# Expert groups of a Flamingo layer: rows turned by the vector engine, odd halves in threes, and the experts' choice and bias additions moved

## The chip, the cores and the metric

The kernel runs on one core of one Trainium2 chip. The metric is the device time of one execution in microseconds (us); the kernel before was timed nine times. The engines are named as the profile names them: PE is the tensor engine's matmuls and PEld its weight loads, DVE the vector engine, ACT the scalar engine, POOL GpSimd, SP the engine that issues most DMAs. All data are 32-bit floats.

## The reference

The layer has two parts, each with a gated residual; x is 8 batches of 512 tokens of 256 features.

```python
x = x + tanh(g_xattn) * (attention(layernorm(x), ctx, ctx, mask) @ wo.T + bo)   # 16 heads of 16
x = x + tanh(g_ffn)   * experts(layernorm(x))

# experts: 8 of them, 256 -> 1024 -> 256, the best 2 of a token
probs = softmax(x_flat @ router_w + router_b)        # 4096 tokens x 8
top_w, top_idx = top_k(probs, 2)
comb = sum(top_w[..., None] * one_hot(top_idx, 8), axis=1)
for e in range(8):
    h = gelu(x_flat @ expert_up[e].T)                # exact gelu
    output += comb[:, e:e+1] * (h @ expert_down[e].T)
```

The mask leaves only the last keys of a sequence open; the kernel reads from the mask that they fit into a window of 128 keys, and then takes the branch `attend_near`. Everything below is about this branch; for any other mask a general branch stands beside it.

## The kernel before, in words

**One schedule for two parts.** `attend_near` (L830) runs the attention batch by batch and mixes the expert layer into it. A batch has four quarters g, and each quarter three slots n: slot 0 weighs the values of the quarter before (`weigh`, L925), slot 1 finds the largest scores for the batch after (`find_tops`, L876), slot 2 lowers queries by them (`lower_tops`, L897). Around these, `between` (L969) fills a plan of (g, n) with the steps of the batches before and after: output projection (`project_out`, L950), layer norms, keys, values and queries. The instructions of an engine run in the order in which the steps issue them; a step waits where its data is not there. The loop is at L1062 to L1101.

**A weighing.** PE multiplies the weights with the values (L933), DVE transposes the result into `raw` (L939), divides it (`n_o`, L942) and, in every second quarter, transposes the heads' outputs (`oT`, L947), which PE projects (L954). GpSimd adds the output bias to a batch's x (`add_bias`, L866): at (2, 0) of the plan, for the first two batches at (1, 0) and (1, 2). `scale_out` (L853) makes that bias once: two columns of `bvT` are spread over 128 by DVE (`bv_rows`, L860) and multiplied with `woT` by PE (L861).

**The choice of experts.** For a finished batch `logits` (L314) multiplies with the router; `route` (L326 to L356), some 25 small DVE operations, takes the softmax and the best two; `place` (L359) counts on GpSimd where each choice goes in a table in memory that has a stretch for every expert; `enter` (L392) scatters the entries (token to read, token to write, weight) by eight indirect DMAs. `route` is at (3, 2); `place` and the scatters follow in the next batch from (0, 2) on. `plan` (L624) turns counts into groups: for each group an expert and a line of the table. Its parts need 3, 6, 8 and 8 finished batches.

**The groups.** A pair is 256 rows of one expert, a single 128. There are 32 pairs (5 + 12 + 15 by part), 4 singles between the last pairs, and 4 more singles in a conditional block. So 36 groups, if the block is not taken. For each group s: SP reads its list from the table (`list_rows`, L707) and its weights, 1 MB up and 1 MB down (`load`, L719); GpSimd gathers its rows (`fetch`, L735), by one indirect DMA per 128 rows; PE turns them by four 128x128 transposes into PSUM and DVE copies that to `xT` (`turn`, L741); PE multiplies with the up weights, two of eight blocks of 128 features at a time, with a Gelu on ACT for each two (`go_up`, L751). `fetch_y` (L764) gathers what the output holds so far for these rows, `go_down` (L770) multiplies with the down weights, adds on DVE (L779) and scatters the rows to the output (L782), one half of 128 rows after the other. Since a token has two experts, the gather of a group's y waits for the scatter of the group before.

**Order of a group.** `compute` (L793) writes group s's steps out: gather of the rows of s + 2, gather of y of s - 1, ups of s, turning of s + 1, downs of s - 1, the list of s + 3, the weights of s + 2. Groups 0 to 3 are worked in amid the attention (`amid`, L1038); from group 4 on the groups run one after the other, each step followed by one of a queue (L1103 to L1114) that holds the last batches' projection, choice, places and scatters.

Of the kernel before, what the change touches and what calls it, by code (L numbers as in the profile page):

```python
# [35 lines left out]

TOKENS = B * S
GROUP = 2 * P
PAIRS = 2 * TOKENS // GROUP
SINGLES = E  # L40

TABLE = TOKENS // GROUP


PARTS = (3, 6, B, B)
ENDS = [-(-(b * S * 2 - E * (GROUP - 1)) // GROUP) for b in PARTS[:2]] + [PAIRS]
SIZES = [ENDS[0], ENDS[1] - ENDS[0], ENDS[2] - ENDS[1], SINGLES]

OFTEN = SINGLES // 2

TABLES = E * TABLE + SIZES[2]
# [4 lines left out]
for _n in range(SIZES[2]):  # L56
    JOBS.append((2, _n))
    if _n % 3 == 2 and _n // 3 < OFTEN:
        JOBS.append((3, _n // 3))
MAIN = len(JOBS)  # L60
JOBS += [(3, n) for n in range(OFTEN, SINGLES)]
# [3 lines left out]
def flamingo_layer(ctx: ExitStack, tc: tile.TileContext, a: dict, out: bass.AP):  # L65
# [11 lines left out]
    table = tc.dram_tile([TABLES * GROUP, ENTRY], I32, name="table")  # L77

    table_parts = dram_disjoint_views(table, B * QT * 2)
    out_parts = dram_disjoint_views(out, 2)  # L80
# [73 lines left out]
    def clear_table(t):  # L154

        many = t.rearrange("p (n c) -> p n c", c=ENTRY)[:, : TABLES * GROUP // P // 11]
        nc.gpsimd.memset(many, 0)
        nc.gpsimd.memset(many[:, :, 0], TOKENS)
        nc.gpsimd.memset(many[:, :, 1], TOKENS - 1)
        n = many.shape[1]  # L160
        nc.sync.dma_start(
            out=table.rearrange("(p r n) c -> p r (n c)", p=P, n=n),
            in_=t[:, : n * ENTRY].unsqueeze(1).to_broadcast([P, TABLES * GROUP // P // n, n * ENTRY]),
        )
# [8 lines left out]
    full_i = mk.tile([P, 2 * TABLE], I32, tag="full_i", name="full_i")  # L173
    nc.gpsimd.iota(full_i, pattern=[[P, 2 * TABLE]], base=0, channel_multiplier=0)
    full = fixed([P, 2 * TABLE], "full")
# [13 lines left out]
    nc.vector.tensor_scalar(filled, iota, float(TOKENS), None, ALU.mult)  # L189
# [422 lines left out]
    def experts(pool, seen, half_bank, bank, row_bank):  # L612
# [6 lines left out]
        tables, loaded, fetched, turned, made, ys = {}, {}, {}, {}, {}, {}  # L619

        def halves(s):
            return 1 if JOBS[s][0] == 3 else 2

        def plan(k):  # L624
            n = SIZES[k]
            single = k == 3
            w = 1 if single else 2
            lines = 2 * TABLE // w

            def planned(shape, name, dtype=F32):  # L630
                return plans.tile(shape, dtype, tag=f"{name}{k}", name=f"{name}{k}")

            def scratch(shape, name):
                return plans.tile(shape, F32, tag=name, name=f"{name}{k}")

            def count():

# [3 lines left out]
                count = scratch([P, E], "count")  # L641
                nc.vector.scalar_tensor_tensor(count, iota, -float(TOKENS), filled, ALU.mult, ALU.add)
                if not single:
                    nc.vector.tensor_scalar(count, count, 1.0 - GROUP if k < 2 else -float(P), None, ALU.add)
                more = scratch([P, E, lines], f"more{lines}")
                nc.vector.tensor_tensor(
                    more, count.unsqueeze(2).to_broadcast([P, E, lines]),
                    full[:, ::w].unsqueeze(1).to_broadcast([P, E, lines]), ALU.is_gt,
                )
                groups = scratch([P, E + 1], "groups")  # L650
                nc.vector.memset(groups[:, E:], 0.0)
                nc.vector.tensor_reduce(groups[:, :E], more, AX.X, ALU.add)
                if k:
                    nc.vector.scalar_tensor_tensor(groups, tables["done"], -2.0 / w, groups, ALU.mult, ALU.add)
                ahead = scratch([P, E + 1, E], "ahead")
                nc.vector.tensor_tensor(
                    ahead, lower, groups[:, :E].unsqueeze(1).to_broadcast([P, E + 1, E]), ALU.mult
                )
                begin = scratch([P, E + 1], "begin")
                nc.vector.tensor_reduce(begin, ahead, AX.X, ALU.add)  # L660

                line = scratch([P, E + 1], "line")
                nc.vector.scalar_tensor_tensor(line, iota_e, float(lines), begin, ALU.mult, ALU.subtract)
                if k:
                    nc.vector.scalar_tensor_tensor(line, tables["done"], 2.0 / w, line, ALU.mult, ALU.add)
                past = scratch([P, n, E + 1], f"past{n}")
                nc.vector.tensor_tensor(
                    past, slot[:, :n].unsqueeze(2).to_broadcast([P, n, E + 1]),  # L670
                    begin.unsqueeze(1).to_broadcast([P, n, E + 1]), ALU.is_ge,
                )
                whose = scratch([P, n], f"whose{n}")
                nc.vector.tensor_reduce(whose, past, AX.X, ALU.add)
                whose_i = planned([P, n], "whose_i", I32)
# [10 lines left out]
                else:  # L686
# [4 lines left out]
                    if k:  # L691
                        nc.vector.tensor_tensor(done, done, tables["done"], ALU.add)
# [684 lines left out]
    with which.Else():  # L1377
        with ExitStack() as att:
            attend_anywhere(att)
        with ExitStack() as exp:  # L1380
# [7 lines left out]
            for count in plans:  # L1388
                count()
# [53 lines left out]
```

## Time and profile before

| what | value |
|---|---|
| time, median of nine (lowest to highest) | 843.58 us (838.62 to 850.68) |
| the profiled execution: its own time, its span | 840.35 us, 838.6 us |
| PE busy in the span | 767.6 us (92%) |
| DVE, ACT, POOL busy | 321.8, 255.3, 312.9 us |
| matmuls down (L776) and up (L758) | 244.1 and 243.9 us |
| transposes of rows (L746), 136 | 21.2 us |
| moved by DMA | 121.58 MB, 145 GB/s |

A line of a timeline has the start and the length in us, the engine, the line of the kernel, the operation, its output and inputs, its shape and how many instructions stand together (x32); in brackets is the idle time of the engine ahead of it and what ended that. Matmuls are pipelined, so neighbouring lengths overlap a little: the pace is read from start to start. The granted clock is the share of full speed that PE was given. Releasers are inferred; an engine's idle time costs something only where a later thing waits for that engine.

The span has three stages: the attention alone (to about 215 us), the attention with groups 0 to 3 between its steps (to about 461 us, with the last batches' remainder at its end), and the groups alone.

### The profile page before, as it was taken

Reading aid. Unit: us, or ns where it says so; the run is one execution under the profiler, and the core shown is the slowest. Engines: PE = TensorE matmul, PEld = TensorE weight load, DVE = VectorE, ACT = ScalarE, POOL = GpSimd, SP = SyncE. Lnnn points to the kernel's source line nnn. Section 1 sums busy time; section 2 is a strip of 40 time slices with the busy share of each in tenths; the row PEclk is TensorE's granted clock in tenths of the full one; section 3 lists DMA queues with packets and bytes.
Section 4 is the critical chain, followed back from the end, with each engine's and each line's share of the span. In section 5 each row is a group of like instructions: output and inputs, shape, how many; then the busy total and the mean of one; then the engine's idle time right before and its main releaser. Section 6 shows DMA issues by size and latency. Waiting matters only on the chain.

```text
span 838.6 us, 11329 instructions
## 1 busy us (share of the span) xinstructions
PE 767.6 (92%) x4090; PEld 568.1 (68%) x4090; DVE 321.8 (38%) x958; ACT 255.3 (30%) x487; POOL 312.9 (37%) x420
## 2 busy tenths in 40 slices
PE   4989989897999999899996999999999999999992
PEld 1443544444456656668785888888898988988882
DVE  6856977878774665632220111111011101101100
ACT  3554636363645344432311111111111111111210
POOL 2030123334453251635463444343343333433332
PEclk9988979999989999999999999999999999999997
DMA  4700202010662223254548466665666765756511
GB/s 153 254 7 2 67 21 79 4 51 4 225 217 85 82 71 109 65 165 142 164 142 301 157 208 214 191 222 173 229 193 211 243 221 178 260 182 224 195 51 36
DMA packets 87909, 121.58 MB, mean 145 GB/s; under 512 B 16797, under 2 KB 71712, under 8 KB 87840
## 3 DMA queue, kind: packets, MB, share of 16 engines
q1 hardware_dynamic: 75184, 93.44, 33.6%
q0 software_dynamic: 11840, 26.76, 10.2%
q8 instruction: 36, 0.59, 0.3%
q10 hardware_dynamic: 816, 0.53, 0.2%
q14 instruction: 33, 0.27, 0.1%
HBM read 101.05 MB, written 20.17 MB: 145 GB/s over the span
## 4 chain that ended last, share of the span: by engine, by line
PE 27%; DMA 12%; issue 8%; POOL 3%; DVE 0%; SPq 0%; POOLq 0%; DVEq 0%
PE o_ps L776 14%; PE h_ps L758 12%; DMA out<-y,listed 5%; DMA y<-out,listed 5%; POOL out L782 1%; POOL y L730 1%; PE x_ps L746 1%; DMA xg<-rows,listed 1%; POOL xg L730 1%; DVE y L779 0%; DMA table<-entries,place_i 0%; DMA listed<-table 0%; POOLq L782 0%; POOL filled L371 0%; POOL place L370 0%
## 5 line engine op out<-in xcount | busy, mean ns | idle before, releaser
L776 PE MATMUL o_ps<-down,hT 128*128 128x256 f32 x1088 | 244.1, 382 | 11.2 <-DVE y L779 10.0
L758 PE MATMUL h_ps<-xT,up 128*128 128x256 f32 (+1 forms) x1152 | 243.9, 368 | 3.5 <-DMA up<-in_upT 1.8
L776 PEld LDWEIGHTS o_ps<-down,hT 128*128 128x128 f32 x1088 | 204.9, 191 | 43.7 <-DVE y L779 11.5
L758 PEld LDWEIGHTS h_ps<-xT,up 128*128 128x128 f32 x1152 | 208.1, 190 | 34.0 <-issue 4.9
L762 ACT ACTIVATE hT<-h_ps 128x512 f32<-128x512 f32 (+1 forms) x144 | 82.0, 573 | 366.1 <-PE h_ps L758 298.2
L779 DVE SCALAR_TENSOR_TENSOR y<-o_ps,listed,y 128x256 f32<-128x256 f32 x68 | 32.6, 482 | 278.3 <-DMA y<-out,listed 128.6
L730 POOL DMA_INDIRECT y<-out,listed x68 | 66.2, 974 | 155.8 <-DMA out<-y,listed 125.7
L782 POOL DMA_INDIRECT out<-y,listed x68 | 68.9, 1013 | 109.9 <-DVE y L779 84.1
L890 DVE TENSOR_REDUCE tops<-t_ps 128x4 f32<-128x512 f32 x128 | 79.1, 680 | 17.1 <-PE t_ps L885 13.8
L920 ACT ACTIVATE n_pT<-w_ps 128x512 f32<-128x512 f32 x128 | 68.2, 596 | 53.6 <-PE w_ps L915 31.9
L730 POOL DMA_INDIRECT xg<-rows,listed x68 | 65.3, 960 | 41.7 <-issue 16.9
L394 POOL DMA_INDIRECT table<-entries,place_i x64 | 62.9, 982 | 25.9 <-issue 16.4
L748 DVE COPY xT<-x_ps 128x512 f32<-128x512 f32 (+1 forms) x36 | 23.7, 658 | 105.3 <-PE x_ps L746 95.2
L915 PE MATMUL w_ps<-ql,km 32*128 32x512 f32 x256 | 58.6, 694 | 1.8 <-DVE tops L890 1.8
L885 PE MATMUL t_ps<-k,q 32*128 32x256 f32 x512 | 42.8, 405 | 3.1 <-issue 1.2
L954 PE MATMUL proj_ps<-woT,oT 128*128 128x256 f32 x128 | 35.6, 418 | 9.8 <-DVE oT L947 9.8
L885 PEld LDWEIGHTS t_ps<-k,q 32*128 32x128 f32 x512 | 26.2, 184 | 24.8 <-issue 14.7
L867 POOL TENSOR_TENSOR x<-x,bo 128x1024 f32<-128x1024 f32 x8 | 18.9, 2372 | 61.6 <-issue 33.6
L933 PE MATMUL n_av<-n_pT,nv 128*32 128x512 f32 x256 | 38.1, 671 | 2.4 <-DVE xT L748 2.3
L939 DVE STREAM_TRANSPOSE raw<-n_av 128x512 f32<-128x512 f32 x32 | 22.8, 712 | 44.4 <-PE n_av L933 26.3
L954 PEld LDWEIGHTS proj_ps<-woT,oT 128*128 128x128 f32 x128 | 24.8, 205 | 21.4 <-DVE oT L947 11.4
L553 PE MATMUL q_ps<-n_xnT,wqT 128*128 128x512 f32 x64 | 33.3, 645 | 0.8 <-ACT n_xnT L282 0.5
(187 smaller groups left out, 549.8 us busy)
## 6 DMA issues: line engine op xcount, KB each, us to landing
up<-in_upT SPq DMA_DIRECT2D x36, 1024.0 KB
down<-in_downT SPq DMA_DIRECT2D x36, 1024.0 KB
out<-x SPq DMA_DIRECT2D x8, 512.0 KB
rows<-xn_f SPq DMA_DIRECT2D x8, 512.0 KB
x<-in_x SPq DMA_DIRECT2D x7, 512.0 KB
table<-none SPq DMA_DIRECT2D x1, 2288.0 KB
xg<-rows,listed POOLq DMA_INDIRECT x68
y<-out,listed POOLq DMA_INDIRECT x68
```

What stands on the lines that cost most here:

```text
L394: nc.gpsimd.indirect_dma_start(out=table_parts[2 * t + i][:, :], out_offset=bass.IndirectOffsetOnAxis(ap=place_i[:, t, i : i + 1], axis=0) ...
L730: nc.gpsimd.indirect_dma_start(out=dst, out_offset=None, in_=src[: seen[JOBS[s][0]], :], in_offset=bass.IndirectOffsetOnAxis(ap=listed[:, ...
L758: nc.tensor.matmul(ps[:, i, :n], lhsT=up[:, dc, (f + i) * P : (f + i + 1) * P], rhs=xT[:, dc, :n], start=(dc == 0), stop=(dc == DC - 1),)
L762: nc.scalar.activation(made[s][:, f : f + 2, :n], ps[:, :, :n], AF.Gelu)
L776: nc.tensor.matmul(ps, lhsT=hT[:, f, h * P : (h + 1) * P], rhs=down[:, f, :], start=(f == 0), stop=(f == FC - 1))
L782: nc.gpsimd.indirect_dma_start(out=out_parts[h][:, :], out_offset=bass.IndirectOffsetOnAxis(ap=listed[:, n, h, 0:1], axis=0), in_=y[:, h, ...
L885: ins = nc.tensor.matmul(ps[j][:, u], lhsT=q[rows_j, c, t * P : (t + 1) * P], rhs=k[rows_j, c], start=True, stop=True)
L890: nc.vector.tensor_reduce(top[:, 2 * tp : 2 * tp + 2, :].rearrange("p t (i x) -> p t i x", i=2)[:, :, :, 32 * j], ps[j], AX.X, ALU.max,)
L915: ins = nc.tensor.matmul(ps[j], lhsT=km[rows_j, c, i, :], rhs=lowered[b, c][rows_j, i, :], start=True, stop=True)
L920: nc.scalar.activation(pT[:, j, :], ps[j], AF.Exp)
L933: ins = nc.tensor.matmul(av[32 * j : 32 * j + 32, :], lhsT=made_of(b)[3][:, 8 * c + 2 * j + r, :], rhs=pT[:, j, :], start=True, stop=True,)
L954: nc.tensor.matmul(ps[:, t - ts[0], :], lhsT=outs[b, c][:, t * P : (t + 1) * P], rhs=w["woT"][:, c, :], start=(c == 0), stop=(c == DC - 1),)
```

## The change

- **Rows turned by DVE.** From group 4 on the rows are no longer turned by PE. `turn_block` makes `xT` by DVE's 32x32 transposes from `xg` straight, in four steps of four instructions, each from 32 partitions to 32 others; the steps are put after the first four ups of the group before. Groups 0 to 3 keep `turn`. The conditional blocks turn their first group by PE.
- **Odd halves in threes.** Singles are gone. An expert's odd half goes with one of its last pairs as a triple of 384 rows; there are four triples, in a pool `wide` that is opened when the queue is empty and the heads' pools are closed. `plan_rest` counts these and the last pairs together, from all 8 batches. The main line has 5 + 12 + 11 pairs and 4 triples; three and four more pairs stand in two nested conditional blocks. A triple's ups go one block of features at a time, with eight Gelus. The table has lines of 128 rows, and the output is written through three views rather than two.
- **The choice a quarter on.** `route` goes from (3, 2) to (0, 2) of the next batch, `place` and the scatters (with the plan behind them) from (0, 2) to (1, 2) on; in the queue at the end likewise.
- **The bias.** `add_bias` first issues a DVE copy of a column of `bo` onto itself, held in the program's order, which the addition on GpSimd waits for; it goes from (2, 0) to (3, 0), the second batch's from (1, 2) to (2, 0). `scale_out` gives PE the column of `bvT` spread by its access pattern, without DVE's two operations.
- **The last group.** Its predecessor's downs come after its first two ups, rather than after all.

```diff
-PAIRS = 2 * TOKENS // GROUP
-SINGLES = E
...
+TRIPLES = 4
+HALVES = TOKENS // P
+SHARE = HALVES + 1
...
+SIZES = [ENDS[0], ENDS[1] - ENDS[0], TRIPLES, 2 * TOKENS // GROUP + E - 1 - TRIPLES - ENDS[1]]
+OFTEN = SIZES[3] - 7
+MORE = OFTEN + 3
...
+LINES = E * SHARE + 2 * SIZES[3]
...
+for _n in range(OFTEN):
+    JOBS.append((3, _n))
+    if _n % 3 == 1 and _n // 3 < TRIPLES:
+        JOBS.append((2, _n // 3))
...
-    out_parts = dram_disjoint_views(out, 2)
+    out_parts = dram_disjoint_views(out, 3)
...
+            pairs, whole = each("pairs"), each("whole")
+            nc.vector.tensor_reduce(pairs, more[:, 0], AX.X, ALU.add)
+            nc.vector.tensor_reduce(whole, more[:, 1], AX.X, ALU.add)
+            left, odd = each("left"), each("odd")
+            nc.vector.tensor_tensor(left, pairs, tables["done"][:, :E], ALU.subtract)
+            nc.vector.tensor_tensor(odd, pairs, whole, ALU.subtract)
...
+            three = each("three")
+            nc.vector.scalar_tensor_tensor(three, left, 2.0, odd, ALU.is_ge, ALU.mult)
+            some, two = each("some"), each("two")
+            nc.vector.tensor_scalar(some, left, 1.0, None, ALU.is_ge)
+            nc.vector.tensor_tensor(two, some, three, ALU.subtract)
...
+            groups = scratch(3, [P, E + 1], "groups")
+            nc.vector.tensor_tensor(groups[:, :E], left, saved, ALU.subtract)
+            begin = plan_pairs(3, groups)
+            for i, end in enumerate((OFTEN, MORE)):
+                tables["extra", i] = planned(3, [P, 1], f"extra{i}_", I32)
+                nc.vector.tensor_scalar(tables["extra", i], begin[:, E:], float(end), None, ALU.is_gt)
...
+        def rows_for(s, name, bufs=None):
+            w = halves(s)
+            if w == 3:
+                return wide[0].tile([P, w, D], F32, tag=f"{name}3", name=f"{name}{s}")
+            return gather.tile([P, w, D], F32, tag=name, name=f"{name}{s}", bufs=bufs)
...
+        def turn_block(s, i):
+            w = halves(s)
+            if i == 0:
+                where, bufs = (wide[0], 1) if w == 3 else (gather, 2)
+                turned[s] = where.tile([P, DC, w * P], F32, tag="xT" if w == 2 else "xT3", name=f"xT{s}", bufs=bufs)
+            src = fetched[s].rearrange("p h (k g x) -> p g k h x", k=DC, x=32)
+            dst = turned[s].rearrange("p k (h i r) -> p i k h r", h=w, r=32)
+            for g in range(4):
+                nc.vector.transpose(dst[32 * g : 32 * g + 32, i], src[32 * i : 32 * i + 32, g])
...
+            m = 512 // (halves(s) * P)
+            return [lambda f=f: go_up(s, f, m) for f in range(0, FC, m)]
...
         def downs(s):
             return [lambda h=h: go_down(s, h) for h in range(halves(s))]
@@ -795,11 +895,17 @@
             steps = [lambda: fetch(s + 2)] if s + 2 < end else []
             if s > first:
                 steps.append(lambda: fetch_y(s - 1))
-            steps += ups(s)
+            up = ups(s)
+            last = downs(s - 1) if s > first else []
             if s + 1 < end:
-                steps.append(lambda: turn(s + 1))
-            if s > first:
-                steps += downs(s - 1)
+                turned_next = turns(s + 1)
+                for step in up:
+                    steps += [step, *turned_next[:1]]
+                    turned_next = turned_next[1:]
+                steps += turned_next + last
+            else:
+                steps += up[:2] + last + up[2:]
...
             for c in range(DC):
-                rows_c = small.tile([P, P], F32, tag="lgT", name=f"bv_rows{c}", bufs=1)
-                tc.keep_in_program_order(nc.vector.tensor_scalar(rows_c, ones, bvT[:, c : c + 1], None, ALU.mult))
-                nc.tensor.matmul(bias_ps, lhsT=rows_c, rhs=w["woT"][:, c, :], start=(c == 0), stop=(c == DC - 1))
+                nc.tensor.matmul(
+                    bias_ps, lhsT=bvT[:, c : c + 1].to_broadcast([P, P]), rhs=w["woT"][:, c, :], start=(c == 0),
+                    stop=(c == DC - 1),
+                )
...
         def add_bias(b):
+            tc.keep_in_program_order(nc.vector.tensor_copy(bo[:, :1], bo[:, :1]))
             nc.gpsimd.tensor_tensor(xs[b], xs[b], bo.unsqueeze(1).to_broadcast([P, QT, D]), ALU.add)
...
-                    put(1, 2, lambda: add_bias(1))
+                    put(2, 0, lambda: add_bias(1))
                 if new > 1:
-                    put(2, 0, bias)
+                    put(3, 0, bias)
             if next_ is not None:
...
-                put(3, 2, route)
...
-            + [lambda: load(5), lambda: turn_rows(4)],
+            + [lambda: load(5), *turns(4)],
...
-            for place, enter, counts in behind_route:
-                plan[0, 2].append(place)
+            for route, place, enter, counts in behind_route:
+                plan[0, 2].append(route)
+                plan[1, 2].append(place)
                 if counts:
-                    plan[0, 2] += enter + counts
+                    plan[1, 2] += enter + counts
                 else:
-                    for where, step in zip(((0, 2), (1, 0), (1, 1), (1, 2)), enter):
+                    for where, step in zip(((1, 2), (2, 0), (2, 1), (2, 2)), enter):
                         plan[where].append(step)
             for g in range(4):
...
-        (place, enter, _), (last, enter_last, counts) = later
-        mixed = [step for pair in zip(rest, [place, *enter] + [wait] * len(rest)) for step in pair]
+        (route, place, enter, _), (route_last, last, enter_last, counts) = later
+        mixed = [step for pair in zip(rest, [route, place, *enter] + [wait] * len(rest)) for step in pair]
         spread = [step for one in enter_last for step in (one, wait, wait)]
-        queue = deque([*mixed, wait, last, *spread, *counts])
+        queue = deque([*mixed, route_last, last, *spread, *counts])
         for s in range(DONE, MAIN):
             for step in compute(s, MAIN, DONE):
                 step()
                 if queue:
                     queue.popleft()()
+                    if not queue:
+                        heads.close()
+                        open_wide()
         compute_extra()
 
 
```

`plan_rest` in short: from the counts it takes, per expert, `pairs` (groups of 256 begun) and `whole` (groups of 256 full over the half), `odd = pairs - whole`, `left = pairs - done`; experts that are odd and have two or more pairs left come first for the four triples, then others with any left; a triple of an odd expert takes the place of two pairs begun. The other pairs are laid out as in `plan` before, now in `plan_pairs`.

## The prediction

> **What bounds the kernel now.** I read the page's engine shares and its 40 slices first, to learn which engine is full and when; then the busy time per stage; then the timeline of TensorE (PE) in the expert stage, for the price of one group; and last the stretches where PE stands still, with the engine that it waits for.
>
> ```profile
> PE 767.6 (92%) x4090; PEld 568.1 (68%) x4090; DVE 321.8 (38%) x958; ACT 255.3 (30%) x487; POOL 312.9 (37%) x420
> ...
> PE   4989989897999999899996999999999999999992
> ```
>
> PE is full from the 23rd slice on, and nearly so from the 11th. By stage (columns: stretch, length, then busy time of PE, PEld, DVE, ACT, POOL, the granted clock, DMA share, GB/s):
>
> ```profile
> 0.00:215.00 215.00, 181.38 (x1053) 89.65 (x1053) 167.03 (x499) 104.27 (x215) 54.57 (x101) 0.93 0.20 65
> 215.00:461.00 246.00, 227.41 (x1282) 162.17 (x1281) 113.20 (x381) 92.69 (x168) 110.90 (x169) 0.97 0.46 148
> 461.00:824.00 363.00, 358.79 (x1756) 316.33 (x1756) 41.08 (x78) 58.37 (x104) 145.36 (x148) 1.00 0.59 195
> ```
>
> In the last stage only 4.2 us are not PE's, so only less PE work shortens it, and DVE has 322 us to give. In the first, PE and DVE lean on each other. PE's timeline (start, length, work, idle before it and what ended that):
>
> ```profile
> 461.04 8.82 PE L776 MATMUL o_ps<-down,hT 128*128 128x256 f32 x32 [6.27 <-DVE y L779]
> ...
> 491.30 7.07 PE L776 MATMUL o_ps<-down,hT 128*128 128x256 f32 x32
> 498.21 7.07 PE L758 MATMUL h_ps<-xT,up 128*128 128x256 f32 x32
> 505.12 0.60 PE L746 MATMUL x_ps<-ident,xg 128*128 128x128 f32 x4
> 505.55 7.07 PE L776 MATMUL o_ps<-down,hT 128*128 128x256 f32 x32
> ...
> 681.84 3.72 PE L776 MATMUL o_ps<-down,hT 128*128 128x256 f32 x16 [1.41 <-DVE y L779]
> ```
>
> From one group's downs to the next's are 14.25 us: 6.91 downs, 6.91 ups, 0.43 for the four transposes of the rows. That last is what the change takes from PE.
>
> **The rows turned by DVE.** The 36 groups hold 68 halves of 128 rows. By the router's counts, worked out from the reference's inputs, the new groups hold 68 too (28 pairs, 4 triples), the seven conditional groups not run. Groups 0 to 3, pairs, keep PE's transposes: 60 halves × 0.216 us (0.43 / 2) = **−12.9**, all on the full engine. DVE gets 16 transposes of 32 partitions × 128 elements per pair, and loses a copy of 0.69. No row has 32 partitions. Nearest: a 128x512 transpose (0.71) above, a 128x4 reciprocal (0.18) below, a 128x128 DVE operation between (0.28, L860). With the elements per partition deciding, I take 0.29: 4.6 us per pair, and 0.97 for its two y additions, within the 13.82 that PE leaves. The cover is gone where 16 of them exceed 12.85, at 0.80 each. The transposes wait for the gathered rows (xg), and behind them on DVE's queue stand the y additions; rows gathered a group ahead leave some 20 us before anybody lacks them.
>
> The Trainium skill ("VectorE: DVE Perf Modes", section "Rules for kernel authors") speaks against this step: a 128×128 transpose belongs on TensorE, since DVE's transposes only 32×32 blocks. The trace's row agrees on PE's cheapness (0.108 us a block) but shows PE full and DVE idle; by the rule this step would be worth nothing or less and the sum would be 12.9 higher.
>
> **The loop through memory.** A group's y is gathered from the output after the previous group's scatter has landed; without PE's transposes this loop has less room.
>
> ```profile
> 513.43 1.01 POOL L782 DMA_INDIRECT out<-y,listed  x1 [1.85 <-DVE y L779]
> 519.79 0.98 POOL L730 DMA_INDIRECT y<-out,listed  x1 [5.36 <-DMA out<-y,listed]
> ...
> 523.64 0.48 DVE L779 SCALAR_TENSOR_TENSOR y<-o_ps,listed,y 128x256 f32<-128x256 f32 x1 [2.94 <-DMA y<-out,listed]
> ```
>
> An addition ending at 513.14 lets the next group's first start at 523.64, 10.5 us later; the second half's gather is issued 1.29 later (521.08), so 11.8, and with 0.8 for the addition and its release 12.6 in all. The room is 13.82: it fits, by 1.2. POOL's six issues are 6 × 1.27 = 7.6. So I cost it at nothing.
>
> **Odd halves in threes.** A single's ups take 3.57 us where half a pair's take 3.46: 4 × 0.11 = **−0.45**. After singles PE waits for the loop: 1.41 (681.84), 0.63 (768.65), 1.23 (784.40), in all 3.27. A triple has 20.7 us for its loop: **−3.3**. Eight Gelus a triple are beside other work, as are the plan's some 40 DVE operations of about 0.2 (as in the choice's rows), 8 us once where DVE has 1 busy us in 9; the wider tiles take the place of the heads' long before the first triple; four groups fewer load 8 MB less.
>
> **The tail.** The last addition (824.40) stood 0.65 for its y, and the last scatter leaves at 826.47, 3.4 after PE's end (823.1). With the previous downs moved in after the first two ups, the last y is there before PE ends: about 0.9 remain, **−2.5**; the 11.1 us from that issue to the end stay.
>
> **The attention part.** Three times PE stands 3.07 us for oT (117.23, 157.41, 196.71):
>
> ```profile
> 117.23 2.93 PE L954 MATMUL proj_ps<-woT,oT 128*128 128x256 f32 x6 [3.07 <-DVE oT L947]
> ```
>
> ```profile
> 109.54 0.18 DVE L330 TENSOR_TENSOR lg<-lg_ps,rb 128x32 f32<-128x32 f32 x1
> ...
> 113.83 2.60 DVE L942 TENSOR_TENSOR n_o<-raw,inv 128x256 f32<-128x256 f32 x1
> 116.47 0.71 DVE L947 STREAM_TRANSPOSE oT<-n_o 128x512 f32<-128x512 f32 x1
> ```
>
> ```profile
> 113.81 2.34 POOL L867 TENSOR_TENSOR x<-x,bo 128x1024 f32<-128x1024 f32 x1 [1.49 <-ACT xn_a L271]
> ```
>
> Two causes lie on DVE's queue ahead of oT: the choice of experts (109.54 to 112.88, 3.35 us), which the change moves a quarter on, and n_o, which took 2.60 beside the bias addition and 0.42 elsewhere (105.47), the addition being what the gate shifts. The Trainium skill ("SBUF — State Buffer", section "SBUF: two separate sides") calls the port pair of DVE and GpSimd an exclusive lock for operations with two SBUF inputs; the rows agree: n_o starts 0.02 us after the addition and lasts as long. After the stall the granted clock is 0.59 from 114 to 126 us and the six projections take 2.93 where at full clock (1.56) 1.4 less; over the three I read some 3 us. scale_out's matmul waits 2.62 for the first of its two DVE operations at 48.81. Gross: 9.2 + 3.0 + 2.6 = 14.8. Against it: the moved choice stands ahead of the next quarter's tops and lowered queries, for which the w_ps matmuls wait; walking DVE's queue on, I get about 1.2 us in each of three batches, 3.6; and with DVE busy 167 of 215 us part of the rest comes back as another wait for it. Ends: 0 (the stall only changes its place) and −18 (that gross and the low clock of 45 to 80 us as well). I take **−8**, near the middle, as the 2.45 us of four tops now met are nearly as large as the wait removed. The gate is a DVE copy of one column, at most 0.18 (the smallest tensor row), 8 × 0.18 = 1.4 on DVE; what queues behind it are that quarter's tops, and it waits only if the bias addition before it, 2.34 us and a quarter or a batch earlier, is unfinished: nothing.
>
> **The place in the table, moved too.** The table's scatters, eight issues of 1.27, go a quarter (about 10 us) later, and POOL's order with them: gathers of rows and y stand behind them, and SP's queue holds the weights' loads behind lists that wait for them. In the first batches there is room: first list 216.0, first rows used 239.67. At the passage to the expert stage there is none: 6.27 (461.04), 1.82 (447.19, weights) and 0.50 idle, 8.6 in all. There the choice moves too. Ends: −8.6 (all gone) and +4 (half a loop of waiting more). My walk of POOL's new order has y of group 6 some 7 us late, yet its PSUM bank free 2.5 us before PE needs it. I take **−2.5**.
>
> **Sum** against the profiled execution, 840.35 us (span 838.6): −12.9 −0.45 −3.3 −2.5 −8 −2.5 = −29.6, so 810.7. The median of nine, 843.58, stands 3.2 above that execution; added: **814**. This kernel's times tell about 0.5%, 4.2 us, from no change.
>
> **The rivals.**
> B, the loop through memory becomes the bound: the gather's landing, now beside DVE's transposes and a denser PE, takes 1.65 us longer than the 12.6, and the pace stays 14.25. For it: room of 1.2 only. Against: POOL's issues keep 0.95 to 1.02 whatever DVE does. 814 + 12.9 = 827.
> C, the moves in the attention part don't do what they say: PE waits for tops at w_ps as long as it did for oT, and the passage costs 4 more. 814 + 8 = 822; with the passage 828, and with each of three batches losing the whole 3.35 of the choice anew 838. Speaks for it: DVE's share there.
> D, the other side: DVE becomes the bound of the expert stage. A pair costs DVE 16t + 0.97, and 24 pairs past group 3 have 13.82. The other steps give 29.6, so slower than before from 24 × (16t − 12.85) = 29.6, t = 0.88 us a transpose. At 0.9, 37 us: 851. Speaks for it: no row of this shape, and that the 128x512 transpose costs 0.71 says that a form can be dear; against: that row is a whole bank in less than 0.80.
> E, more: the passage's stall goes wholly (6.1 more) and the attention part gives its 15 (7 more): 801.
>
> **How the numbers follow.** Forecast 0.55 (own range 806 to 820), B 0.12, C 0.15, D 0.09, E 0.09. The range 799 to 835 leaves out D, C's upper end and what exceeds E. Faster: 0.55 + 0.12 + 0.09 + 0.11 of C = 0.87; the same: C's other 0.04; slower: D, 0.09.
>
> **What would show it.** No x_ps matmuls past group 3, and 13.8 us from downs to downs. Transposes from xg on DVE near 0.3 us each; over 0.8, D. An idle time of PE ended by y's addition in each group: B. In the first 215 us, the waits of 3.07 for oT gone and n_o at 0.42 throughout; waits at w_ps for tops above 3 us instead: C. The idle time near 461 tells the passage; the last scatter within 1 us of PE's end the tail. A conditional group run would cost a pair, 14 us, and would make all this wrong.

## The result, and the profile after

The changed kernel takes 884.0 us (median of 20 runs, 876.6 to 889.6) where the kernel before, in 62 runs beside it, takes 841.8: a ratio of 1.051, 95% interval 1.049 to 1.053. It is slower by 42 us, and the forecast of 814, with a range to 835, is wrong in sign. The profiled execution took 885.17 us with a span of 883.5.

The page of the changed kernel, the lines that answer to those shown of before:

```profile
PE 761.6 (86%) x3842; PEld 547.8 (62%) x3842; DVE 431.5 (49%) x1390; ACT 257.6 (29%) x489; POOL 312.8 (35%) x420
...
PE   4999988788899898496979999986959977996993
```

PE has 248 instructions fewer, as it should, and DVE 110 us more work, at 49% still far from full. But PE, which was full from the 23rd slice on, now has a hole of 4 tenths in the 17th and others down to 5 tenths from the 28th on, nearly to the end. The stages (stretch, length, busy time of PE, PEld, DVE, ACT, POOL, granted clock, DMA share, GB/s):

```profile
0.00:215.00 215.00, 182.57 (x1113) 89.26 (x1117) 163.15 (x517) 111.21 (x230) 52.32 (x100) 0.94 0.21 68
215.00:461.00 246.00, 209.41 (x1151) 149.75 (x1144) 132.92 (x472) 85.29 (x151) 108.60 (x165) 0.93 0.40 135
461.00:824.00 363.00, 325.56 (x1401) 273.28 (x1400) 131.12 (x393) 54.81 (x96) 136.01 (x139) 0.95 0.52 171
```

The first stage does more work than before in the same time (1113 matmuls for 1053). In the second and third, which are the same stretches of time as before and not the same work, PE is busy for 18 and 33 us less, at a lower clock. What PE waited for (engine, line, releaser: us in total, times, the longest):

```profile
PE o_ps L872 <- DVE y L875: 42.5, 8, 9.7
PE xnT_ps_f L283 <- DVE y L875: 11.8, 1, 11.8
...
PE lg_ps L330 <- DVE y L875: 7.2, 1, 7.2
```

All three end with the addition of y on DVE: 42.5 + 11.8 + 7.2 = 61.5 us. In the kernel before, the waits for y were 10.3 us (the line below, and 0.3 in one other):

```profile
PE o_ps L776 <- DVE y L779: 10.0, 5, 6.3
```

PE's timeline of the changed kernel shows where:

```profile
485.69 7.07 PE L872 MATMUL o_ps<-down,hT 128*128 128x256 f32 x32
492.60 7.07 PE L854 MATMUL h_ps<-xT,up 128*128 128x256 f32 x32
499.50 7.07 PE L872 MATMUL o_ps<-down,hT 128*128 128x256 f32 x32
...
585.32 8.86 PE L872 MATMUL o_ps<-down,hT 128*128 128x256 f32 x32 [2.77 <-DVE y L875]
...
608.74 9.36 PE L872 MATMUL o_ps<-down,hT 128*128 128x256 f32 x32 [7.65 <-DVE y L875]
617.94 10.48 PE L854 MATMUL h_ps<-xT,up 128*128 128x384 f32 x32
```

Between 472 and 575 us a pair takes 13.81 us, as forecast. The stalls begin when DVE comes to the first triple's transposes, ahead of that triple's ups (128x384), and come again at the transposes of each other triple (9.23 us at 658, 9.71 at 734, 7.25 at 807). The larger ones are followed by matmuls at a lower clock: 9.36 us for work of 7.07 at 608.74, where the granted clock is 0.76, against 1.00 from 472 to 575 us. The other two waits, 11.8 and 7.2 us, end at 372 and 415 us, where DVE holds transposes of groups 5 and 7. Why the addition is late is seen on DVE and on GpSimd, at the first triple:

```profile
569.71 4.11 DVE L843 STREAM_TRANSPOSE xT<-xg 32x128 f32<-32x128 f32 x13
584.00 0.75 DVE L843 STREAM_TRANSPOSE xT<-xg 32x192 f32<-32x192 f32 x2 [10.18 <-DMA xg<-rows,listed]
584.78 0.48 DVE L875 SCALAR_TENSOR_TENSOR y<-o_ps,listed,y 128x256 f32<-128x256 f32 x1
585.30 4.58 DVE L843 STREAM_TRANSPOSE xT<-xg 32x192 f32<-32x192 f32 x12
589.91 0.48 DVE L875 SCALAR_TENSOR_TENSOR y<-o_ps,listed,y 128x256 f32<-128x256 f32 x1
```

```profile
572.57 0.99 POOL L807 DMA_INDIRECT y<-out,listed  x1 [6.62 <-DMA out<-y,listed]
573.86 0.97 POOL L807 DMA_INDIRECT y<-out,listed  x1 [0.30 <-issue]
575.14 0.95 POOL L807 DMA_INDIRECT xg<-rows,listed  x1 [0.30 <-issue]
576.40 0.95 POOL L807 DMA_INDIRECT xg<-rows,listed  x1 [0.30 <-issue]
577.65 0.95 POOL L807 DMA_INDIRECT xg<-rows,listed  x1 [0.30 <-issue]
585.55 1.01 POOL L878 DMA_INDIRECT out<-y,listed  x1 [6.95 <-DVE y L875]
```

(The first DVE line is the end of a pair's 16 transposes.) As the steps are written, the transposes of a group come behind the additions of the group three before it. The text on the kernel before says that an engine runs its instructions in the order in which the steps issue them; the trace shows that this does not hold for DVE. Counting the additions, two for a pair, the regular rounds have a group's transposes just ahead of the additions of the group three before it. That costs nothing, since the gather of these rows is issued ahead of the gather of that y. But the transposes of the triple (32x192) stand one group further ahead, before the additions of the group four before it. Why the order changes there, no run shows. The triple's transposes wait for rows whose gather GpSimd issues after the gather of that y, 575.14 to 577.65, and which land 6.35 us after the last issue. DVE stands still for 10.18 us, and the additions behind the first two and the next twelve transposes end at 585.26 and 590.39. In the regular round before, the addition came at 561.77 for a gather issued at 558.55, 3.2 us; here 584.78 - 572.57 = 12.2 us. The scatter leaves late by as much, the next y is gathered after that scatter, the next rows after that y, and the next transposes wait for those rows: the delay feeds itself until the order on DVE changes back.

### The profile page after: what moved, and what is told of

Read it like the earlier page. It is cut to its first block, busy times and chain, and to the rows that moved or that the text cites. A ratio compares the mean times of both kernels' runs of the same rounds, so it can differ in the third digit from the quotient of the medians.

```text
span 883.5 us, 11155 instructions
## 1 busy us (share of the span) xinstructions
PE 761.6 (86%) x3842; PEld 547.8 (62%) x3842; DVE 431.5 (49%) x1390; ACT 257.6 (29%) x489; POOL 312.8 (35%) x420
## 5 line engine op out<-in xcount | busy, mean ns | idle before, releaser
L872 PE MATMUL o_ps<-down,hT 128*128 128x256 f32 x1088 | 257.7, 397 | 42.6 <-DVE y L875 42.5
L872 PEld LDWEIGHTS o_ps<-down,hT 128*128 128x128 f32 x1088 | 215.8, 200 | 85.0 <-DVE y L875 46.6
L843 DVE STREAM_TRANSPOSE xT<-xg 32x128 f32<-32x128 f32 (+1 forms) x448 | 139.9, 312 | 215.8 <-DMA xg<-rows,listed 201.1
L854 PEld LDWEIGHTS h_ps<-xT,up 128*128 128x128 f32 x1024 | 194.6, 191 | 42.3 <-issue 2.3
L1035 PE MATMUL w_ps<-ql,km 32*128 32x512 f32 x256 | 55.2, 698 | 3.4 <-DVE tops L1010 1.4
L1005 PEld LDWEIGHTS t_ps<-k,q 32*128 32x128 f32 x512 | 26.7, 188 | 22.6 <-issue 10.5
L1074 PE MATMUL proj_ps<-woT,oT 128*128 128x256 f32 x128 | 31.5, 389 | 0.0
```

The source lines that it names most:

```text
L843: nc.vector.transpose(dst[32 * g : 32 * g + 32, i], src[32 * i : 32 * i + 32, g])
L854: nc.tensor.matmul(ps[:, i, :], lhsT=up[:, dc, (f + i) * P : (f + i + 1) * P], rhs=xT[:, dc, :], start=(dc == 0), stop=(dc == DC - 1),)
L872: nc.tensor.matmul(ps, lhsT=hT[:, f, h * P : (h + 1) * P], rhs=down[:, f, :], start=(f == 0), stop=(f == FC - 1))
L1005: ins = nc.tensor.matmul(ps[j][:, u], lhsT=q[rows_j, c, t * P : (t + 1) * P], rhs=k[rows_j, c], start=True, stop=True)
L1035: ins = nc.tensor.matmul(ps[j], lhsT=km[rows_j, c, i, :], rhs=lowered[b, c][rows_j, i, :], start=True, stop=True)
L1074: nc.tensor.matmul(ps[:, t - ts[0], :], lhsT=outs[b, c][:, t * P : (t + 1) * P], rhs=w["woT"][:, c, :], start=(c == 0), stop=(c == DC - 1),)
```

## The experiments

Theory A: the order on DVE, as just read. Theory B: the triples, with three gathers and scatters in a turn. Theory C: DVE's reading of 32 partitions disturbs GpSimd, in whatever order. All ratios are to the kernel before on the same chip. The chips differed: the kernel before took 839.8 us beside the first four, 822.5 beside the next four and 839.2 beside the last four, so only ratios are compared across sets.

**The order pinned.** Each transpose of rows is held behind what was written before it for DVE. The work stays the same: both pages count 3842 instructions on PE, 1390 on DVE and 420 on GpSimd, and GpSimd issues the gathers of rows and of y in the same sequence in both traces.

```diff
-                nc.vector.transpose(dst[32 * g : 32 * g + 32, i], src[32 * i : 32 * i + 32, g])
+                tc.keep_in_program_order(
+                    nc.vector.transpose(dst[32 * g : 32 * g + 32, i], src[32 * i : 32 * i + 32, g])
+                )
```

> The changed kernel with one thing added: each of DVE's transposes of rows is held behind what was written before it for DVE, so those of group s + 1 stand behind the y additions of group s - 2 and ahead of those of s - 1, and never a group earlier. Theory A (order): in the changed kernel the transposes of group s + 2 stand ahead of the y additions of s - 1 around each triple and in groups 4 to 7, and wait for rows whose gather is issued behind that very y's gather; so the additions, the scatter, the next y and PE follow late. Then PE's waits that end with a y addition fall from 61.5 us (42.5 + 11.8 + 7.2) to below 15, and the low clock behind them (some 14 us) goes: 815 us, between 806 and 830. Theory B (the triples themselves: three gathers and three scatters in a turn of the loop through memory): the waits stay at the triples, 860 or more. Theory C (DVE's reading of 32 partitions slows GpSimd's gathers, whatever the order): no change, 875 to 890.

Measured: 821.0 us, ratio 0.976 (0.971 to 0.982). In the pinned trace each group's transposes come behind the additions of the group three before it, as written. (In the changed kernel they were displaced at the triples by one group more than the expectation says, as counted above.) Theory A's number: 1.051 becomes 0.976 with the same work in another order on DVE. B is refuted as the main cause, since the triples are still there, and so is C, since the same transposes are: GpSimd's issues of gathers last 976 ns for y in the changed kernel and 974 in the one before. (The Trainium skill, "SBUF — State Buffer", section "SBUF: two separate sides", warns that some DVE operations keep GpSimd from writing its descriptors; no run here shows that for these transposes.) The waits, and DVE at the first triple:

```profile
PE h_ps L856 <- DMA up<-in_upT: 7.6, 1, 7.6
...
PE o_ps L874 <- DVE y L877: 2.3, 2, 2.0
```

```profile
576.23 0.48 DVE L877 SCALAR_TENSOR_TENSOR y<-o_ps,listed,y 128x256 f32<-128x256 f32 x1 [9.03 <-DMA y<-out,listed]
579.59 0.48 DVE L877 SCALAR_TENSOR_TENSOR y<-o_ps,listed,y 128x256 f32<-128x256 f32 x1 [2.88 <-DMA y<-out,listed]
579.99 6.10 DVE L844 STREAM_TRANSPOSE xT<-xg 32x192 f32<-32x192 f32 x16
```

The triple's 16 transposes now come after both additions, in one run of 6.10 us, and end at 586.09; PE's triple begins at 588.50 without a wait.

**The pinned kernel again**, as a measure on the last chip.

> The pinned kernel once more, on the same chip as the three beside it, as their measure: the ratio to the kernel before that it had (0.976, 0.971 to 0.982) is expected again.

Measured: 821.8 us, 0.981 (0.977 to 0.986). The intervals overlap.

**Rows turned by PE, all else as changed.**

```diff
...
-                turned_next = turns(s + 1)
-                for step in up:
-                    steps += [step, *turned_next[:1]]
-                    turned_next = turned_next[1:]
-                steps += turned_next + last
+                steps += [*up, lambda: turn(s + 1), *last]
...
-            + [lambda: load(5), *turns(4)],
+            + [lambda: load(5), lambda: turn_rows(4)],
```

Left out above is `turn`, which takes a triple's rows in two steps of three 128x128 transposes, each copied by DVE.

> The changed kernel with the rows of all groups turned by PE as before (a triple's in two steps of 3 x 128 columns through PSUM, each copied by DVE); triples, attention part and tail as changed. Theory A: no transposes stand ahead of the additions, so the waits for y go and PE has its 12.9 us of transposes back: 828 us, 818 to 840. Theory B: the triples' waits stay, 865 or more. Theory C cannot be told from A here.

Measured: 825.8 us, 0.981 (0.976 to 0.986). As A has it: with triples and without DVE's transposes the waits for y are one of 4.8 us, at the passage to the expert stage. PE is busy for 759.9 us against the pinned kernel's 746.6: the 13 us of transposes. The medians differ by 4.8 us only, and their intervals overlap; how much of the 13 reaches the end is not settled by this pair.

**DVE's transposes alone, on the kernel before.**

```diff
...
-            steps += ups(s)
-            if s + 1 < end:
-                steps.append(lambda: turn(s + 1))
-            if s > first:
-                steps += downs(s - 1)
+            turned_next = turns(s + 1) if s + 1 < end else []
+            for step in ups(s):
+                steps += [step, *turned_next[:1]]
+                turned_next = turned_next[1:]
+            if s > first:
+                steps += downs(s - 1)
...
```

> The kernel before with DVE's transposes alone (from group 4 on, after the first four ups); pairs and singles, attention part, bias and tail as before. In this program's order on DVE no group's transposes cross the y additions of the group two before it in the last stage. Theory A: faster by the 12.9 us of PE's transposes, or some less where groups 4 to 7 have their transposes between other steps: 830 us, 826 to 838. Theory C: as slow as before or slower, 842 or more. Theory B (triples): as A.

Measured: 839.7 us, 0.998 (0.994 to 1.002): no gain. The expectation missed; it counted crossings in the last stage and not those among groups 4 to 7. There the same thing happens, without any triple. DVE's and PE's timelines:

```profile
408.27 5.08 DVE L758 STREAM_TRANSPOSE xT<-xg 32x128 f32<-32x128 f32 x16 [13.55 <-DMA xg<-rows,listed]
413.39 0.88 DVE L791 SCALAR_TENSOR_TENSOR y<-o_ps,listed,y 128x256 f32<-128x256 f32 x2
```

```profile
413.93 0.47 PE L328 MATMUL lg_ps<-ident,lgT 128*128 128x128 f32 x1 [9.33 <-DVE y L791]
```

The rows come late because their gather stands behind the table's scatters on GpSimd (401.5 us), two y additions stand behind the transposes, and PE loses 9.33 us. PE's waits for y are 20.9 us in all (9.7 + 9.3 + 1.9), 10.6 more than in the kernel before: most of the gain of some 12.9.

**The attention part alone, on the kernel before** (choice and places a quarter on, bias gated and moved, bias made without DVE).

```diff
         def add_bias(b):
+            tc.keep_in_program_order(nc.vector.tensor_copy(bo[:, :1], bo[:, :1]))
...
-                    put(2, 0, bias)
+                    put(3, 0, bias)
...
-                put(3, 2, route)
...
+                plan[0, 2].append(route)
+                plan[1, 2].append(place)
```

> The kernel before with the attention part's changes alone: the choice of experts and its places a quarter on, the bias additions gated and moved, the bias made without DVE. The changed kernel reaches the first rows' turning at 226.5 us against 239.7 before. If that holds alone and to the end: 830 us (842 less 13), and the wait of PE at the passage to the expert stage tells what of it is given back there, since the last choice and its table entries come later: 834 if 4 us are given back. If the attention part had no share in it: 842.

Measured: 832.7 us, 0.992 (0.988 to 0.996): 6.7 us, with 3.4 to 10 as the interval's ends. The waits for oT are gone and n_o takes 0.59 at most; the first rows are turned at 227.4 us rather than 239.7. Of these 12 us 5 to 6 are given back. PE's waits between there and the passage have new names (4.0 for DVE's raw, 3.4 for ACT's logits), and the passage keeps 5.5 + 1.5 of its 8.6. The place in the table moves in this kernel too, so the 6.7 us stand for the prediction's two terms together, the attention part (-8) and the passage (-2.5).

**Singles in place of triples, all else as pinned.** The kernel before with the attention part, the pinned transposes and the tail.

Against the pinned kernel (the last pairs are kind 3 and triples kind 2 there, pairs kind 2 and singles kind 3 here):

```diff
...
-for _n in range(OFTEN):
-    JOBS.append((3, _n))
-    if _n % 3 == 1 and _n // 3 < TRIPLES:
-        JOBS.append((2, _n // 3))
+for _n in range(SIZES[2]):
+    JOBS.append((2, _n))
+    if _n % 3 == 2 and _n // 3 < OFTEN:
+        JOBS.append((3, _n // 3))
...
-            m = 512 // (halves(s) * P)
-            return [lambda f=f: go_up(s, f, m) for f in range(0, FC, m)]
+            return [lambda f=f: go_up(s, f) for f in range(0, FC, 2)]
...
```

> The kernel before with the changed attention part, DVE's transposes held in the program's order, and the last downs after two ups, but pairs and singles as before: the pinned kernel without triples. By the prediction's terms triples are worth 0.45 + 3.3 us: 825 beside the pinned kernel's 821. If triples carry a cost of their own even in order (Theory B's remainder), it is as fast as that kernel or faster: 821 or less. The singles' short turns of the loop should show as waits of PE for a y addition, 3 us or more in all.

Measured: 813.5 us, 0.990 (0.986 to 0.993), slower than the pinned kernel's 0.976 and 0.981 by 0.8 to 1.3%, across chips, where 0.5% was forecast. On its own chip the two kernels with triples and pinned transposes that are told below take 800.4 and 800.8 us. The four singles cost 9.7 us of waits. Waits for y had been expected, but these are others; the profile names no releaser for them, and DVE shows it:

```profile
603.04 5.03 DVE L759 STREAM_TRANSPOSE xT<-xg 32x128 f32<-32x128 f32 x16
```

```profile
608.17 7.15 PE L772 MATMUL h_ps<-xT,up 128*128 128x256 f32 x32 [1.54 <-issue]
```

The transposes are held behind the additions of the pair ahead of the single, the second of which starts at 602.64 and had waited for its y. They end at 608.07, and the ups that need them start 0.1 us later. So with the order pinned a short group leaves DVE too little time, and triples avoid that; without DVE's transposes (the attention part alone) no single is followed by a wait at all.

**Weights asked for ahead of lists.** SP's queue in the pinned kernel:

```profile
396.97 0.37 SPq L801 DMA_DIRECT2D up<-in_upT  x1
397.59 0.37 SPq L802 DMA_DIRECT2D down<-in_downT  x1
425.97 0.37 SPq L791 DMA_DIRECT2D listed<-table  x1
427.41 0.05 SPq L801 DMA_DIRECT2D up<-in_upT  x1
```

```diff
-            if s + 3 < end:
-                steps.append(lambda: list_rows(s + 3))
             if s + 2 < end:
                 steps.append(lambda: load(s + 2))
+            if s + 3 < end:
+                steps.append(lambda: list_rows(s + 3))
```

> The pinned kernel with the weights of group s + 2 asked for ahead of the list of s + 3 on SP's queue, rather than behind it. In the pinned kernel SP's queue stands from 398 to 426 us behind a list that waits for the table's scatters, and PE then waits 7.63 us for the up weights at 432. If that order is what is left of the passage: 7 us less, 814, and no wait for up weights above 1 us. If rows or y are late at the same place anyway, the wait changes its name and the time stays: 819 to 822.

Measured: 794.8 us, 0.967 (0.964 to 0.971), the best ratio of all, and no wait for up weights. The pinned kernel itself was not run on this chip. Beside the next two kernels below, which were, and which keep the old order of loads but differ in the choice or the bias, it is 0.6 to 0.7% faster. So the longest wait at the passage in the pinned kernel was no longer for y but for a weights load that was queued behind a list.

**The choice back in its old slots; and the bias back in its old slots, without the gate.** Each alone, on the pinned kernel.

```diff
+                put(3, 2, route)
...
-                plan[0, 2].append(route)
-                plan[1, 2].append(place)
+                plan[0, 2].append(place)
```

```diff
-            tc.keep_in_program_order(nc.vector.tensor_copy(bo[:, :1], bo[:, :1]))
...
-                    put(3, 0, bias)
+                    put(2, 0, bias)
```

> The pinned kernel with the choice of experts and its places back in their old slots, the bias additions still gated and moved. If the choice ahead of the heads' outputs on DVE is what PE waited for (3.07 three times): 9 us more, 830. If it was the bias addition's slowing of n_o (2.2 us each time): 3 more at most, 824, as the gate remains; some is given back at the passage by earlier lists, up to 8, which would bring it below 821.

> The pinned kernel with the bias additions back in their old slots and without the gate, the choice still a quarter on. If the addition's slowing of n_o holds without the choice ahead: 2.2 us three times, 827. If only the choice mattered: 821 to 822. n_o's longest duration tells whether the addition falls beside it.

Measured: 0.974 (0.971 to 0.978) and 0.973 (0.970 to 0.976): the same, and no slower than the pinned kernel's 0.976 and 0.981. With the old choice and the moved bias, PE's waits for the heads' outputs are:

```profile
PE proj_ps L1076 <- DVE oT L1069: 4.3, 5, 0.9
```

at most 0.9 where it was 3.07, and 4.3 us in all where they were 9.8. With the old bias and the moved choice there are none, and n_o takes 1.18 at the longest, against 2.61. Both moves address the same wait, and either one removes more than half of it. The gate by itself does not keep the bias addition clear of n_o: with the old choice and the gate in place, one n_o takes 2.52 us, from 215.23, beside an addition that starts at 215.11.

**Loads ahead of lists, with group 4 turned by PE.**

```diff
-            + [lambda: load(5), *turns(4)],
+            + [lambda: load(5), lambda: turn_rows(4)],
```

> The pinned kernel with weights ahead of lists, and with the rows of group 4 turned by PE, as the first four are. There PE waited 3.6 us at 345.6 for DVE's transposes of group 4, held behind a y addition. If that wait is all that the pin costs there: 0.43 us of PE for 3.6, so 3 us (0.4%) faster than that kernel's ratio of 0.967, 0.963 to 0.965. If the next wait takes its place: no difference.

Measured: 816.6 us, 0.975 (0.971 to 0.980). On this chip the pinned kernel has 0.981, so the two edits together bring 0.6% (821.8 to 816.6 us), no more than loads ahead of lists seem to bring by themselves: what group 4 adds can't be told. The waits for xT fall from 6.5 to 2.5 us. This kernel and the one with loads ahead of lists are both faster than the kernel before and the changed one.

**Loads ahead of lists, with the choice in its old slots** (the diff of the choice above, and that of the loads).

> The pinned kernel with weights ahead of lists, and with the choice and its places in their old slots. With the bias additions moved, PE's waits for the heads' outputs are at most 0.9 us with the old slots, against 3.07 in the kernel before; so the later choice is worth little once the addition is out of the way, and the earlier lists give about 4 us at the first rows: ratio 0.960 to 0.967. If the later choice is worth its own 3.35 us of DVE in each batch: 0.975 or more.

Measured: 823.3 us, 0.985 (0.978 to 0.991), not the gain that was expected. It is 0.9% above the kernel just told, with intervals that overlap; where the choice is best put is left open within that 1%.

**Without the conditional groups.** Leaves out the seven extra groups and the reading of their condition, from the pinned kernel.

```diff
-        compute_extra()
```

> The pinned kernel without the conditional groups at the end: leaves out the seven extra groups, which these inputs don't need, and the reading of their condition. From PE's end to the end of the span are 15.5 us in the kernel before, in the changed one and in the pinned one, though the last scatter leaves 3.4, 0.8 and 0.8 us after PE's end. If the conditional part sets that end: 5 us or more less between PE's end and the span's. If the last rows' landing and the program's end set it: 15 us again.

Measured: 817.6 us, in one execution only, with a span of 815.8. The end of the work:

```profile
796.32 10.52 PE L874 MATMUL o_ps<-down,hT 128*128 128x256 f32 x48
...
807.64 0.98 POOL L880 DMA_INDIRECT out<-y,listed  x1 [2.44 <-POOLq L1499]
```

From PE's end (806.84) to the end of the span are 9.0 us, against 15.4 to 15.6 in the kernel before, the changed and the pinned one: the conditional part sets that end.

## Why the prediction was wrong

**The step that failed** is the end of "The rows turned by DVE": "The transposes wait for the gathered rows (xg), and behind them on DVE's queue stand the y additions; rows gathered a group ahead leave some 20 us before anybody lacks them." It named the queue and then asked who lacks the rows. The ups do have 20 us. But DVE, while it waits for the rows, also holds the additions, and these are wanted at once, as they free PE's bank and start the loop through memory. The order had been read as regular, one group's transposes and then the additions; in groups 4 to 7 and around each triple the transposes of a later group stood ahead of the additions too, and that was costed at nothing. It was worth 61.5 us of waits, 51.2 more than before, and about 14 us of matmuls at the lower clock after them (1.8 + 2.3 + 3.1 + 2.9 + 2.0 + 2.1 above their usual lengths; the kernel before has one such place, 1.8 at 461). Against 840.35: -12.9 for PE's transposes, -6.7 for the attention part and the passage, +51.2, +12.4 makes 884, and 885.17 was measured. This is a rough balance: it leaves out smaller waits that came and went, such as 7.0 us for ACT's x2T, so that it comes out within 1 us is partly luck. The firmer number is the pin's, from 1.051 to 0.976 by the order.

Point by point:

- **A transpose's price.** 0.30 us for a pair's and 0.37 for a triple's, where 0.29 was taken. Rival D, which needed 0.88, was the only one that ended slower, and its mechanism did not occur: DVE was busy for 131 of 363 us in the last stage. The right direction would have come from the wait that was dismissed.
- **The loop through memory.** The pace of 13.82 held wherever the order was regular (13.81 measured); rival B is refuted.
- **The 12.9 us, and the rule against the change.** PE's busy time fell by 13.3 between the kernel with PE's turning and the pinned one. In the pinned kernel the forecast's mechanism is at work; with the whole change it comes to 0.976 to 0.981 where the forecast had 814 / 843.6 = 0.965. The rule of the Trainium skill ("VectorE: DVE Perf Modes", section "Rules for kernel authors") that such a transpose belongs on TensorE was no worse a guide than the sum here: 0.981 with PE's turning, 0.976 to 0.981 with DVE's in order.
- **Stalls after singles, -3.3.** Not the singles alone: in the kernel with the attention part alone, where PE turns the rows, the same four singles are followed by no wait. What triples are worth showed only under the pin, some 10 us of waits.
- **The tail, -2.5.** It measured 0: the last scatter did move to 0.8 us after PE's end, but PE's end to the span's stayed 15.5 (15.4 in the changed kernel, 868.1 to 883.5), since the conditional part sets it. The 11.1 us after the last scatter had been taken for a constant; it was what was left of another one.
- **The attention part, -8, and the passage, -2.5.** Measured together, -6.7 for the -10.5: the direction was right, the size some 4 us too large; that some of the stall would only change its place held too. In the changed kernel n_o takes 0.58 us at the longest, against 2.61, and no bias addition runs beside it there. The exclusive lock that the Trainium skill states ("SBUF — State Buffer", section "SBUF: two separate sides") agrees. But the prediction took the gate to be what shifts the addition, and the 2.52 us with the gate and the old choice show that the gate alone does not ensure it.
- **The passage by itself.** PE's waits there fell by about 1 us, from 6.27 + 1.82 to 5.5 + 1.5. In the pinned kernel the longest wait there is for the up weights (7.6), no longer for y, and for it the order of SP's queue was the cause: with the loads ahead of the lists it is gone.

## What to carry to other kernels

When work is moved to an idle engine, its price is the small part; ask, for each instruction that may wait there, what stands behind it on that engine's queue, and when the waited-for data are issued relative to what the others need. A transfer that is early enough for its own consumer is late if that consumer's queue also holds somebody who is wanted now. And where the order on an engine is not held to that of the program, read it for every kind of group, not for the regular one: four irregular groups in 32, and the first few, undid a gain that was real in all the others.

## What was not expected of the hardware

The kernel before took 822.5 us on one chip and 839 to 842 on others; its executions do not overlap (817.4 to 827.0 us on the one, 830.5 to 847.1 on another). In two kernels whose steps are the same up to there (the pinned one on another chip, and that with loads ahead of lists), the granted clock from 100 to 150 us was 0.93 and 1.00, and the first rows were turned at 223.8 and 214.4 us. So the clock was not granted alike to the same steps. Why is not shown, with one profile of each; only ratios measured side by side were comparable.

The conditional part, not taken, still costs about 6.5 us at the end (15.5 less 9.0, the latter from one execution).
